# Sixteen copies of the experts' weights in DRAM, a new account of transfers in the build, and other constants of the order

## The chip, the core and the metric

The kernel runs on one core of one Trainium2 chip. The core has five engines, each with its own stream of instructions, which it works off in order: TensorE (matrix products; PE in the profile, PEld its weight loads), VectorE (DVE), ScalarE (ACT), GpSimd (POOL) and SyncE (SP), which here does nothing but issue transfers. Semaphores order the engines among each other. All transfers go out on SyncE's one queue and are carried by 16 DMA engines. The metric is the device time of one execution in microseconds (us); three executions of the kernel before took 1351.25 to 1354.19 us, median 1353.21.

## What is computed

The input is x, 8 sequences of 512 tokens with 128 channels, in fp32. Four blocks follow each other, each added to its input:

```python
x = x + mamba(layernorm(x))      # in-projection, short convolution, Silu, state scan, out-projection
x = x + ffn(layernorm(x))        # mixture of 8 experts
x = x + attention(layernorm(x))  # 16 heads of 8, chunks of 10 with 25 to the left
x = x + ffn(layernorm(x))        # the same mixture, with the same weights
```

The experts take most of the work. All eight compute every token, and their outputs are summed with a weight per token and expert:

```python
router_probs = softmax(x @ w_router);  gate_weights = softmax(x @ w_gating / 0.1)
h = silu(x @ w_gate[e]) * (x @ w_up[e]);  expert_out[e] = h @ w_down[e]      # 128 -> 512 -> 128
cw = router_probs * gate_weights;  cw = cw / (sum(cw) + 1e-9)
out = sum over e of expert_out[e] * cw[..., e]
```

## The kernel before

**The experts' stream.** `ffn_stream` runs over the pass k (0, 1), the sequence b (0 to 7), the expert e (0 to 7) and four chunks f of 128 of the 512 hidden channels. Tokens lie along the free dimension, 512 columns. For each chunk TensorE makes g and u, then, some chunks later, adds to y. Each of the three is made of three products (`matmul3`), since every operand is split into a high and a low part of type fp32r: high times high, low times high, high times low. `hidden` turns g and u into the operand of y: ScalarE takes Silu of g (h<-g), VectorE multiplies by u (h<-u,h), ScalarE or VectorE rounds to the high part (a cast, h<-h), and GpSimd or VectorE subtracts to get the low part (h<-h,h). g, u and y live in accumulator banks, of which the experts may hold six (MOST) and one more. While the function tables on ScalarE are those of the exponential, some of the first Silus are computed through tanh.

**The weights of the experts** in fp32 come in as "stage" tiles; ScalarE casts the high half and GpSimd (VectorE at times) subtracts for the low half, 24 tiles in all, during the first sequence.

**The first sequence** starts in two halves of 256 tokens (`passes`, `first_halves`): experts 0 to SPLIT-1 run first on the first half of the tokens, then on the second half, and the others on all 512. Before the first product TensorE makes "warm" products, which compute nothing; while it waits early in the stream it makes "idle" ones (`keep_warm`).

**The weights per token.** `ffn_prep` normalises the tokens, computes the logits (lps), turns them (rps), takes the exponential (pr), and has cw, 128 tokens by NT blocks by NE experts. It transposes cw on TensorE (cps), VectorE copies it out (cwt), SyncE stores it in DRAM (cwd), and `spreads` loads the row of one expert into all 128 partitions (cwb), two tiles in turn, one expert ahead. `weighted` then has VectorE multiply y by cwb, and GpSimd add that to acc. In the profile the names of such tiles have the letter f after the first part (cwd_f, pr_f).

**Other work beside the stream.** Mamba (tiles with an m), preparation of the experts, and attention (tiles with an a) are generators, called lanes. Each yields the engine that it needs next, and when it may go on.

**What sets the order.** The order of instructions is fixed while the kernel is built. `Clock` keeps an account of when each engine will be free: `cost` gives a duration for each operation and `run` adds it up; for a transfer `run` works out when the data will have landed. `Lanes.tick` takes, among all lanes that could go on by the account, the one with the earliest start, less an allowance. The constants steer this choice: SIDE and JOIN say how long a result must have been ready before work beside the stream takes TensorE; PRESS, HELD and SECOND are allowances; MAMBA_DUE and PREP_DUE say how early a lane counts as due; LATE bounds how long an exponential waits for a table that is already loaded; WARM_GAP is the gap by the account from which an idle product is put in, and WARM_TO how far into the stream (in sequences) this is done; SPLIT is told above. So any change of the account or of a constant can move instructions anywhere in the program, on all engines.

ScalarE's function tables hold sets of functions; a change between Silu, exponential and logarithm takes a table load (ACT_TABLE_LOAD). One part of the Mamba work loads the set with the exponential and the logarithm (mdelta, mdec).

Nearly all instructions are recorded by one helper, so that they share one line in the profile (269); they are told apart by the names of their tiles.

Of the kernel before, what the change touches and what calls it, by code (L numbers as in the profile page):

```python
# [8 lines left out]
F32 = mybir.dt.float32  # L9
# [9 lines left out]
P = 128  # L19
B, L, DIM = 8, 512, 128  # L20
NT = L // P
# [3 lines left out]
NE, FF = 8, 512  # L25
# [62 lines left out]

TABLES = {AF.Silu: (18,), AF.Exp: (0, 6), AF.Ln: (6,), AF.Tanh: (0, 18)}
INF = float("inf")  # L90
LAGS = {"T": 0.2, "A": 0.15, "V": 0.15, "P": 0.08}
TO_PE = 0.11
SAME = 0.125
AHEAD = 0.2
EDGE = 0.1
FIRST = 0.6
LATE = 0.3
SIDE = 0.5
JOIN = 2.0
JOIN_DUE = 0.0  # L100
JOIN_MAX = 6.0
JOIN_ATT = 3.0
# [2 lines left out]
OTHERS = 4  # L105
AT_FIRST = 7
WARM = 3.5
WARM_GAP = 0.25
WARM_TO = 1.5
SECOND = 0.2  # L110
PRESS = 0.4
HELD = 0.18
MAMBA_DUE = 0.9
PREP_DUE = 0.9
ATT_LEAD = 2.5
EARLY = 5
SPLIT = 4
EARLIEST = 2 * (DEPTH + 1)


# [8 lines left out]
class Clock:  # L129
# [105 lines left out]
    def run(self, key, name, out, args, kw, after, wait):  # L235
        c = self.cost(key, name, out, args, kw)
        start = max(self.end[key] + wait, after, self.now if key == "T" else self.based(key))
        if key == "T":
            if start > self.end["T"] + 2.4:
                self.cold = start  # L240
            if start < self.cold + 3.4:
                c *= 2
        if key in "VP" and self.shares(key, name, out, args):
            start = self.with_port(start, c)
        self.end[key] = start + c
        if key == "S":
            start = max(start, self.now)
            row = out.shape[-1]
            rows = out.shape[0] * size(out) // row
            each = max(row * (2 if out.dtype == BF16 else 4), 512)  # L250
            move = rows * each / 200e3
            self.moved = max(self.moved, start + c + 0.8) + move
            return self.moved + 0.6 + move
        self.hop[key] = start + c
        return start + c + LAGS[key]

# [121 lines left out]
def block_kernel(ctx: ExitStack, tc: tile.TileContext, x, pack_a, pack_b, pack_c, w_qkv, mask, mask_t, w_o,  # L378
# [4 lines left out]
    pe = Engine(nc.tensor, "T", clock)  # L383
# [3 lines left out]
    sp = Engine(nc.sync, "S", clock)  # L387

    const = ctx.enter_context(tc.tile_pool(name="const", bufs=1))
    dram = ctx.enter_context(tc.tile_pool(name="dram", bufs=1, space=DRAM))  # L390
    lnp = ctx.enter_context(tc.tile_pool(name="lnp", bufs=LNB))
    fp = ctx.enter_context(tc.tile_pool(name="fp", bufs=2))
# [10 lines left out]
    done = {}  # L403
# [73 lines left out]
    ident = const.tile([P, P], F32, name="ident")  # L477
# [545 lines left out]
    def ffn_prep(k, b, xc, t0=0, nt=NT):  # L1023

        nm = f"f{k}_{b}_{t0}"
        cols = slice(t0 * P, (t0 + nt) * P)

        def halves():
            if t0 == 0:
                ready[k, b] = [fp.tile([P, L], F32R, tag=f"xt{i}", name=f"xt{i}_{nm}") for i in range(2)], 0  # L1030
            return [t[:, cols] for t in ready[k, b][0]]

        if (k, b, t0) == (0, 0, 0):
            done["quiet"] = 0.0
        *_, xf = yield from normalised(xc, nm, halves, nt, t0 + nt == NT, quick=nt < NT, plain=True)
        if (k, b, t0) == (0, 0, 0):
            done.pop("quiet", None)
            done["calm"] = 0.0
        if t0 == 0:
            done["cw", k, b] = dram.tile([NT, NE, P], F32, tag="cwd", name=f"cwd_{nm}", bufs=3), 0.0, 0  # L1040
        cwd = done["cw", k, b][0]
        ready[k, b] = ready[k, b][0], cols.stop
        wr, = routes

        lps = yield from side([P, P], f"lps_{nm}")
        for t in range(nt):
            e = pe.matmul(lps[32 * t : 32 * t + 32], wr, xf[:, t * P : (t + 1) * P], start=True, stop=True)
        lanes.give("ln", e)
        yield "V"
        n = 32 * nt  # L1050
        lt = fp.tile([P, P], F32, tag="lt", name=f"lt_{nm}", bufs=1)
        freed(dve.tensor_copy(lt[:n], lps[:n]))
        yield "T"
        rps = yield from side([P, NT, 32], f"rps_{nm}")
        pe.transpose(rps.rearrange("p t c -> p (t c)")[:, :n], lt[:n], ident[:n, :n])
        yield "V"
        pr = fp.tile([P, 2 * NT, NE], F32, tag="pr", name=f"pr_{nm}")
        s8 = fp.tile([P, 2 * NT], F32, tag="s8", name=f"s8_{nm}")
        pr, s8 = pr[:, : 2 * nt], s8[:, : 2 * nt]
        prv = pr.rearrange("p (t s) e -> p t s e", s=2)  # L1060
        s8v = s8.rearrange("p (t s) -> p t s", s=2)
        logits = rps[:, :nt, : 2 * NE].rearrange("p t (s e) -> p t s e", s=2)
        dve.tensor_reduce(s8v, logits, AX.X, ALU.max)
        yield "V"
        freed(dve.tensor_tensor(prv, logits, s8v[:, :, :, None].to_broadcast([P, nt, 2, NE]), ALU.subtract))

        yield lambda: clock.table in TABLES[AF.Exp] or pos[0] >= k * B + b - LATE
        yield "A"
        act.activation(pr, pr, AF.Exp)
        if (k, b) == (0, 0) and t0:  # L1070
            clock.hold = clock.now


        yield "V"
        cw = fp.tile([P, NT, NE], F32, tag="cw", name=f"cw_{nm}")[:, :nt]
        s4 = fp.tile([P, NT], F32, tag="s4", name=f"s4_{nm}")[:, :nt]
        z = fp.tile([P, NT], F32, tag="z", name=f"z_{nm}")[:, :nt]
        dve.tensor_reduce(s8, pr, AX.X, ALU.add)
        pool.tensor_tensor(cw, prv[:, :, 0], prv[:, :, 1], ALU.mult)
        yield "V"  # L1080
        dve.tensor_reduce(s4, cw, AX.X, ALU.add)
        pool.tensor_tensor(z, s8v[:, :, 0], s8v[:, :, 1], ALU.mult)
        pool.tensor_scalar(z, z, 1e-9, 1.0, ALU.mult, ALU.mult)
        yield "P"
        pool.tensor_tensor(s4, z, s4, ALU.add)
        yield "V"
        dve.reciprocal(s4, s4)
        yield "P"
        pool.tensor_tensor(cw, cw, s4[:, :, None].to_broadcast([P, nt, NE]), ALU.mult)
        yield "T"  # L1090
        cps = yield from side([NT * NE, P], f"cps_{nm}")
        n = nt * NE
        pe.transpose(cps[:n], cw.rearrange("p t e -> p (t e)"), ident)
        yield "V"
        cwt = fp.tile([NT * NE, P], F32, tag="cwt", name=f"cwt_{nm}")
        freed(dve.tensor_copy(cwt[:n], cps[:n]))
        yield "S"
        e = sp.dma_start(out=cwd[t0 : t0 + nt].rearrange("t e p -> (t e) p"), in_=cwt[:n])
        done["cw", k, b] = cwd, e, cols.stop

    pos = [0.0]
# [21 lines left out]
    def ffn_stream():  # L1123
# [73 lines left out]
        def spreads():  # L1197

            for k in range(2):
                for b in range(B):  # L1200
                    todo = passes(k, b)
                    for i, (e, cs) in enumerate(todo):
# [3 lines left out]
                        cwd, there, _ = done["cw", k, b]  # L1206
                        yield "S", there
                        spread.append(e)
                        n = cs.stop - cs.start
                        cwb = fp.tile([P, L], F32, tag="cwb", name=f"cwb{k}_{b}_{e}_{cs.start}", bufs=2)[:, :n]  # L1210
                        state["cwb", (k, b, e, cs.start)] = cwb, sp.dma_start(
                            out=cwb.rearrange("p (t q) -> p t q", q=P),
                            in_=cwd[None, cs.start // P : cs.stop // P, e, :].to_broadcast([P, n // P, P]),
                        )

        def chunks(cs):
# [63 lines left out]
        for k in range(2):  # L1280
            for b in range(B):
                todo = passes(k, b)
                for n, (e, cs) in enumerate(todo):
# [8 lines left out]
                    for f in range(0, NFC, n_chunks):  # L1292
                        nm = f"{k}_{b}_{e}_{cs.start}_{f}"
# [567 lines left out]
```

## Time and profile before

| | before |
|---|---|
| median of three executions | 1353.21 us |
| the profiled execution, its own time | 1351.62 us |
| its span, first to last instruction | 1349.8 us |
| mean granted clock of TensorE | 0.996 |
| busy share PE / DVE / ACT / POOL | 98 / 77 / 71 / 70% |
| share of the 16 DMA engines' time | 33.9% |
| table loads on ScalarE | 125 (109 and 16 by line), 1.28 us each |
| broadcasts of the weights per token (cwb<-cwd_f) | 132: 124 of 256 KB, 8 of 128 KB |

A row of the profile names line, engine, operation, what it writes and reads with the shape, the count, then busy time and the mean length of one, then the idle time of the engine before it and what ended that. Products on TensorE overlap, so a row's length is not its cost; the cost of one is the distance to the start of the next. Idle products count as busy time. The chain of waits follows the work that ended last back to its beginning.

### The profile page before, as it was taken

How to read it: one execution, taken by the hardware profiler on the slowest of the kernel's cores; microseconds unless marked ns; L12 is line 12 of the kernel's file. 1: busy time of each engine (PE TensorE's matmuls, PEld its weight loads, DVE VectorE, ACT ScalarE, POOL GpSimd, SP SyncE). 2: the span in 40 equal slices, each digit the busy share in tenths (PEclk: the TensorE clock that was granted, in tenths of full speed). 3: DMA queues.
4: the chain of work that ended last, by engine and by line, in shares of the span. 5: the costliest groups of instructions: out<-in, count | busy, mean ns of one | idle time of the engine just before them, and what ended most of it. 6: DMA issues, size and time to landing. Idle time of an engine off the chain costs nothing.

```text
span 1349.8 us, 29533 instructions
## 1 busy us (share of the span) xinstructions
PE 1328.9 (98%) x10261; PEld 1053.3 (78%) x10261; DVE 1036.8 (77%) x3114; ACT 964.7 (71%) x1694; POOL 940.4 (70%) x1042
## 2 busy tenths in 40 slices
PE   7999999999999999999999999999999999999998
PEld 7877778788788877777777777777777777778887
DVE  6887888688888867898788887888888787855443
ACT  7768576867787556777777777777877767765654
POOL 5877576776767757666766767767677676777776
PEclk9999999999999999999999999999999999999999
DMA  3321304232112242344345444454544434222111
GB/s 126 95 72 38 87 24 101 62 81 73 45 48 56 63 85 54 73 97 118 79 103 111 99 106 100 104 109 89 118 91 104 119 71 88 61 69 55 40 40 40
DMA packets 230861, 107.75 MB, mean 80 GB/s; under 512 B 86417, under 2 KB 226616, under 8 KB 230712
## 3 DMA queue, kind: packets, MB, share of 16 engines
q1 hardware_dynamic: 230712, 105.87, 33.9%
q8 instruction: 81, 1.33, 0.4%
q14 instruction: 68, 0.56, 0.1%
HBM read 77.64 MB, written 27.79 MB: 78 GB/s over the span
## 4 chain that ended last, share of the span: by engine, by line
PE 89%; POOL 3%; ACT 3%; issue 3%; DVE 2%; DMA 0%; POOLq 0%; DVEq 0%
PE u L269 25%; PE y L269 25%; PE g L269 25%; PE ao L269 2%; PE aw L269 2%; PE as L269 2%; POOL h L269 1%; PE mo L269 1%; PE aqk L269 1%; ACT h L269 1%; DVE h L269 1%; PE mde L269 1%; PE aout L269 1%; PE yp L269 1%; ACT L269 1%
## 5 line engine op out<-in xcount | busy, mean ns | idle before, releaser
L269 POOL TENSOR_TENSOR h<-h,h 128x512 fp32r<-128x512 f32 x492 | 640.0, 1310 | 279.0 <-ACT h L269 219.4
L269 PE MATMUL u<-xt_f,wu 128*128 128x512 f32 (+1 forms) x1584 | 451.5, 395 | 3.5 <-ACT h L269 2.7
L269 PE MATMUL g<-xt_f,wg 128*128 128x512 f32 (+1 forms) x1584 | 448.3, 393 | 2.1 <-ACT h L269 1.9
L269 PE MATMUL y<-h,wd 128*128 128x512 f32 (+1 forms) x1584 | 445.5, 392 | 1.4 <-POOL h L269 0.8
L269 DVE TENSOR_TENSOR h<-u,h 128x512 f32<-128x512 f32 x420 | 285.9, 686 | 157.5 <-PE u L269 109.3
L269 ACT ACTIVATE h<-g 128x512 f32<-128x512 f32 x512 | 303.4, 597 | 123.2 <-PE g L269 100.1
L269 ACT CAST h<-h 128x512 fp32r<-128x512 f32 x437 | 268.4, 619 | 171.2 <-DVE h L269 169.6
L269 PEld LDWEIGHTS g<-xt_f,wg 128*128 128x128 f32 x1584 | 288.5, 189 | 70.3 <-ACT h L269 3.0
L269 PEld LDWEIGHTS y<-h,wd 128*128 128x128 f32 x1584 | 288.3, 188 | 70.2 <-POOL h L269 1.4
L269 PEld LDWEIGHTS u<-xt_f,wu 128*128 128x128 f32 x1584 | 286.6, 189 | 71.7 <-ACT h L269 4.1
L269 POOL TENSOR_TENSOR acc<-acc,cwb 128x512 f32<-128x512 f32 (+1 forms) x114 | 148.0, 1298 | 52.5 <-DVE cwb L269 33.8
L269 ACT ACT_TABLE_LOAD x109 | 139.8, 1283 | 24.7 <-PE g L269 23.2
L269 DVE CUSTOM_DVE_ANT_0 amasked<-as,maskq 128x60 f32<-128x60 f32 x640 | 95.4, 213 | 5.0 <-PE as L269 4.8
L269 DVE TENSOR_TENSOR cwb<-y,cwb 128x512 f32<-128x512 f32 (+1 forms) x116 | 77.5, 668 | 16.0 <-PE y L269 14.4
L269 DVE TENSOR_TENSOR apt<-aw,maskk 125x400 f32<-125x400 f32 (+2 forms) x160 | 88.1, 570 | 0.0
L269 DVE SCALAR_TENSOR_TENSOR h<-h,g 128x512 f32<-128x512 f32 x92 | 62.3, 681 | 27.0 <-ACT h L269 26.6
L269 ACT ACTIVATE apt<-apt 125x400 f32<-125x400 f32 (+2 forms) x160 | 81.5, 540 | 0.4
L269 DVE SCALAR_TENSOR_TENSOR h<-u,h 128x512 f32<-128x512 f32 x92 | 62.6, 683 | 3.3 <-PE g L269 0.5
L269 DVE DVE_READ_ACCUMULATOR2_ANT amx<- 128x1 f32 x640 | 52.1, 81 | 0.0
L269 DVE CAST h<-h 128x512 fp32r<-128x512 f32 x75 | 48.8, 651 | 1.2
L269 DVE COPY v<-avr 125x128 f32<-125x128 f32 (+2 forms) x40 | 25.7, 644 | 26.4 <-PE ao L269 26.4
L269 PEld LDWEIGHTS ao<-apt,v 125*32 125x32 f32 (+2 forms) x1280 | 27.4, 109 | 14.6 <-DVE h L269 4.4
(205 smaller groups left out, 1239.5 us busy)
## 6 DMA issues: line engine op xcount, KB each, us to landing
cwb<-cwd_f SPq DMA_DIRECT2D x124, 256.0 KB
aqd<-apc SPq DMA_DIRECT2D x32, 192.0 KB
ks<-aqd SPq DMA_DIRECT2D x48, 93.8 KB
x_fo<-x SPq DMA_DIRECT2D x16, 256.0 KB
aqd<-apc SPq DMA_DIRECT2D x32, 128.0 KB
x_f<-x SPq DMA_DIRECT2D x15, 256.0 KB
qs<-aqd SPq DMA_DIRECT2D x48, 75.0 KB
aod<-aos SPq DMA_DIRECT2D x24, 100.0 KB
```

The lines of the kernel that those rows point to most:

```text
L269: f(*args, **kw)
```

## The change

The weights of the tokens are stored in DRAM expert by expert, not block by block, so that the 512 weights of one expert are one piece of 2 KB. The store writes them sixteen times, and partitions 8r to 8r+7 of cwb read copy r. In the first sequence, which is prepared in two halves, there is one copy. To this end cw is laid out with the experts outside on chip as well, and the transpose follows that order.

In the build's account a transfer used to begin 0.8 us after its issue and to land 0.6 us and once more its moving time after its move; now it begins after 0.6 us and lands 0.8 us after its move. Eleven constants have other values.

```diff
+COPIES = 16
-LATE = 0.3
-SIDE = 0.5
-JOIN = 2.0
+LATE = 0.4
+SIDE = 0.7
+JOIN = 3.0
...
-WARM_GAP = 0.25
-WARM_TO = 1.5
-SECOND = 0.2
-PRESS = 0.4
-HELD = 0.18
-MAMBA_DUE = 0.9
-PREP_DUE = 0.9
+WARM_GAP = 0.5
+WARM_TO = 2.5
+SECOND = 0.1
+PRESS = 0.2
+HELD = 0.05
+MAMBA_DUE = 1.0
+PREP_DUE = 0.8
...
-SPLIT = 4
+SPLIT = 5
...
-            self.moved = max(self.moved, start + c + 0.8) + move
-            return self.moved + 0.6 + move
+            self.moved = max(self.moved, start + c + 0.6) + move
+            return self.moved + 0.8
...
-            done["cw", k, b] = dram.tile([NT, NE, P], F32, tag="cwd", name=f"cwd_{nm}", bufs=3), 0.0, 0
+            copies = COPIES if nt == NT else 1
+            done["cw", k, b] = dram.tile([copies, NE, NT, P], F32, tag=f"cwd{copies}", name=f"cwd_{nm}", bufs=3), 0.0, 0
...
-        cw = fp.tile([P, NT, NE], F32, tag="cw", name=f"cw_{nm}")[:, :nt]
+        cw_rows = fp.tile([P, NE * NT], F32, tag="cw", name=f"cw_{nm}")[:, : NE * nt]
+        cw = cw_rows.rearrange("p (e t) -> p t e", e=NE)
...
-        pe.transpose(cps[:n], cw.rearrange("p t e -> p (t e)"), ident)
+        pe.transpose(cps[:n], cw_rows, ident)
...
-        e = sp.dma_start(out=cwd[t0 : t0 + nt].rearrange("t e p -> (t e) p"), in_=cwt[:n])
+        if nt == NT:
+            e = sp.dma_start(
+                out=cwd.rearrange("r e t p -> (e t) r p"), in_=cwt[:, None, :].to_broadcast([n, COPIES, P])
+            )
+        else:
+            e = sp.dma_start(out=cwd[0, :, t0 : t0 + nt, :], in_=cwt[:n])
...
-                            out=cwb.rearrange("p (t q) -> p t q", q=P),
-                            in_=cwd[None, cs.start // P : cs.stop // P, e, :].to_broadcast([P, n // P, P]),
+                            out=cwb,
+                            in_=cwd[:, None, e, cs.start // P : cs.stop // P, :]
+                            .rearrange("r o t q -> r o (t q)")
+                            .to_broadcast([cwd.shape[0], P // cwd.shape[0], n]),
```

## The prediction

> **What bounds the kernel now.** I read the page's busy times first, then busy time by stage, then TensorE and ScalarE in order of time where a stage falls short.
>
> ```profile
> PE 1328.9 (98%) x10261; PEld 1053.3 (78%) x10261; DVE 1036.8 (77%) x3114; ACT 964.7 (71%) x1694; POOL 940.4 (70%) x1042
> L269 ACT ACT_TABLE_LOAD x109 | 139.8, 1283 | 24.7 <-PE g L269 23.2
> ```
>
> TensorE sets the time; the others have a quarter of the span free. So a transfer or an operation elsewhere counts only where TensorE stands. The stages, first whole, then the opening in detail (columns: stretch, its length, then PE, PEld, DVE, ACT, POOL busy, granted clock, DMA share, GB/s):
>
> ```profile
> 0.00:40.00 40.00, 32.34 (x212) 28.64 (x213) 27.31 (x71) 26.53 (x57) 22.12 (x33) 0.96 0.41 126
> 300.00:500.00 200.00, 200.00 (x999) 160.18 (x998) 163.36 (x324) 140.31 (x241) 132.15 (x134) 1.00 0.26 62
> 900.00:1100.00 200.00, 199.62 (x2108) 155.88 (x2099) 166.62 (x619) 152.40 (x275) 140.18 (x165) 1.00 0.47 102
> ...
> 51.60:59.10 7.50, 7.44 (x50) 5.66 (x48) 5.04 (x11) 6.69 (x12) 5.71 (x6) 1.00 0.34 90
> 67.00:71.00 4.00, 2.85 (x12) 1.47 (x11) 3.55 (x13) 3.92 (x6) 1.37 (x2) 0.98 0.02 7
> 71.00:76.00 5.00, 4.88 (x22) 4.00 (x21) 3.91 (x9) 4.99 (x12) 4.27 (x6) 0.68 0.25 63
> ```
>
> From 300 us on TensorE is full and nothing is to be had but cheaper products. The slack lies in the opening, and busy time hides it, because "idle" products (fillers that compute nothing) count as busy. In order of time (start, length, engine, what):
>
> ```profile
> 51.63 1.17 PE L269 MATMUL idle<-sel 128*128 128x256 f32 x4
> 55.94 1.17 PE L269 MATMUL idle<-sel 128*128 128x256 f32 x6
> 68.38 2.14 PE L269 MATMUL idle<-sel 128*128 128x256 f32 x5 [0.86 <-DVE cwt_f L269]
> 70.58 1.46 PE L269 MATMUL u<-xt_f,wu 128*128 128x256 f32 x6
> ```
>
> To size it I count useful work. In the chain three 512-column products take 0.70 us (0.233 each), six 256-column ones 0.72 (0.12 each); the others go by the median from start to start. The first gate product starts at 34.31 us, the first of the second half of the tokens at 59.10: 24.8 us for 20.7 of work, 4.1 lost. From there to expert 5 at 99.59: 40.5 us for 31.8 of work, 8.7 lost. What holds TensorE at 67 to 71 is ScalarE:
>
> ```profile
> 61.09 1.28 ACT L269 ACT_TABLE_LOAD   x1
> 62.39 0.23 ACT L269 ACTIVATE pr_f<-pr_f 128x32 f32<-128x32 f32 x1
> 62.64 1.28 ACT L269 ACT_TABLE_LOAD   x1
> 63.93 0.60 ACT L269 ACTIVATE h<-g 128x512 f32<-128x512 f32 x1
> 64.55 1.28 ACT L569 ACT_TABLE_LOAD   x1
> 65.84 1.30 ACT L269 ACTIVATE mdelta<-mdelta 128x512 f32<-128x512 f32 x2
> 67.17 1.95 ACT L269 ACTIVATE mdec<-mdelta,nega 128x512 f32<-128x512 f32 x3
> 69.15 0.72 ACT L269 ACTIVATE mdelta<-mdelta,nega 128x512 f32<-128x512 f32 x1
> 69.89 1.28 ACT L269 ACT_TABLE_LOAD   x1
> 71.19 1.57 ACT L269 ACTIVATE h<-g 128x512 f32<-128x512 f32 x3
> ```
>
> Four table loads in ten microseconds: only one Silu of the experts runs between 60 and 71 us, the accumulator banks stay full, TensorE starves, and its clock falls to 0.68 for the next 5 us.
>
> **The change, part by part.** The programs of both versions, engine by engine, give the counts.
>
> *Transfers of the weights.* 132 broadcasts of 256 KB become 133 whose pieces are 2 KB (1 KB for half rows), not 512 B. In the landing events of the trace the 512-byte form takes 4.86 us (median) after its issue, a broadcast of the same size in 2 KB pieces (aall_over) 2.93; I expect about 3. In 15 of the 16 preparations the store grows from 16 to 256 KB: from 1.7 us towards the 2.5 of the 256 KB store avd. SP issues these in order, so cwb of expert 0 and whatever is queued behind it come about 1 us later, once per sequence. Who waits? VectorE waits for cwb 0.5 us in the whole span, and TensorE's waits for transfers are three rows of 0.7. So the gain is 0 to 2.1 us, the loss at most 1 us of SP per sequence, hidden by the next cwb being loaded one expert ahead. I take 0. If that cover were gone, each of the 15 could lose 1 us; the 0.5 us row says it is not.
>
> The Trainium skill, "DMA: Bandwidth & Descriptors" (the rule on using all 16 engines), says that an outermost dimension under 16, such as a leading broadcast, confines a transfer to that many engines. It would speak against fewer copies; sixteen just meets it, and no run here shows the other case.
>
> *First product (A).* GpSimd forms the low half of a weight from 28.93 for 1.30 us and only at 30.31 starts the norm that VectorE had ready at 29.57. In the new program ScalarE casts the first weight of that group ahead of four exponentials and a table load, not behind them (GpSimd had idled 8.62 us for this cast, up to 26.36), and the last cast of the group comes 0.8 us sooner for GpSimd: 0.7 gained, all that VectorE allows. The filler ahead of the first gate product (33.89 to 34.31) goes: 0.4. A = -1.1; bounds 0 and -1.7.
>
> *Filling the wait for the second half (B).* SPLIT 5 runs expert 4 on the first half too: 36 products at 0.12, 4.3 us of work before the second half is needed, in the place of 14 fillers, of which 4 are left. The price: 36 products of 0.233 become 72 of 0.12, +0.3. Expert 4's weights are needed some 35 us earlier (its first product started at 86.7); their casts move ahead, and one low half goes from GpSimd (1.29) to VectorE (0.69 for an operation of this form). Of 4.1 us lost I take half: B = -2.1 + 0.3 = -1.8; bounds -3.8 and +0.3.
>
> *Behind it (C).* The exponential of the second half's router moves into the stretch whose table already holds it: two of the four loads go, 2.57 us of ScalarE. Against that, two weight casts and one h cast (3 x 0.52) and this exponential (0.23) now stand in the Silu-free stretch, which grows from 6.64 us (64.55 to 71.19) to 6.64 + 1.8 = 8.4. But ScalarE enters it less late: the two Silus ahead of it were 5.7 us apart (58.21 and 63.93), and now nothing stands between them. GpSimd does the two h's ahead of three weights (3.8 us) instead of behind two. Of 8.7 us I take 3.0; bounds -8 and +1.8.
>
> *Clock.* The gap before a filler is put in doubles, to 0.5. At 68.38 to 70.58 five fillers ran, and the clock fell to 0.68 all the same, so these fillers bought nothing: 0. The Trainium skill, "TensorE: Matmul & The Clock Gate" (Part 1), has a window of about 3.4 us of low activity before half rate; by it single gaps of 0.5 are harmless too, and the sum would be the same.
>
> *Order of the rest (D, E).* Table loads go from 125 to 131, but 19 to 15 in the first two sequences and 106 to 116 after them. Ten at 1.28 us are 12.8 us of ScalarE, where it is busy 70 to 76% and TensorE is full: taken at 0. "ScalarE: Activation LUTs" of the skill (What ACT_TABLE_LOAD costs) adds a drain, 2.66 us in all; the rows show 1.30 from the load's start to the next operation (61.09 to 62.39), so the row holds. The stalls at 174 and 263 us (1.9 and 1.6) stand at Silu-free stretches of ScalarE; by the rows' lengths the old program has eight of over 4 us from expert 6 of the first sequence on, the new one ten. D = +1.0, half a stall for each of the two; bounds -4 and +5. Changes between 512-column products and small ones fall from 104 to 99 and, with the row-tiled ones, from 79 to 76, at 0.1 to 0.15 us: E = -1.0 with the cheaper neighbours, bounds 0 and -2. The end of the program is the same on all engines.
>
> **Sum.** -1.1 - 1.8 - 3.0 + 1.0 - 1.0 = -5.9 us on the profiled execution's 1351.62 (span 1349.8): 1345.7. That execution is 1.6 below the median of the three runs, 1353.21, so 1347.3.
>
> **Rivals.**
> 1. *ScalarE's Silu-free stretches decide (slower).* Stock for TensorE lasts some 4 us: the stretch of 6.3 us at 169.68 to 175.95 cost 1.9 us and then a slow clock. If the 8.4 us stretch keeps B and C from coming, and half of the ten later loads come through (6.4 us), the sum is -1.1 + 0.3 - 1.0 + 6.4 = +4.6: 1357.8. For it: six loads more, one stretch longer. Against: no stall at any of the 106 later loads but 0.85 us at 521. It decides from the fourth later load on that comes through whole (-1.8 + 4 x 1.28 = +3.3).
> 2. *GpSimd sets the pace of the opening (no change).* Between 71 and 90 us the chain of waits runs through GpSimd, which has 24 weight halves of 1.29 us to make. Then B and C only move the wait: -1.1 + 0.3 - 1.0, 1351.4.
> 3. *All of the slack comes (much faster):* -1.7 - 3.8 - 8 - 2 = -15.5: 1337.7.
> 4. *The copies don't speed the transfers up.* Same account, since they count at 0.
>
> **How the numbers follow.** My sum 0.50, rival 1 0.20, rival 2 0.19, rival 3 0.11; rival 4 lies inside all. 0.2% is 2.7 us, about what a measurement of this kernel can tell. Faster 0.61 (my sum, rival 3), same 0.19, slower 0.20. The range, 1340.5 to 1356.5, cuts off half of rival 3 and the upper half of rival 1; for my sum alone it would be 1342 to 1351.
>
> **What would show it.** After: the first gate product near 33 us; one or two fillers before the second half; two table loads, not four, around the second Mamba sequence and no 3 us hole there; expert 5 of the first sequence some 6 us earlier; from 300 us on a full TensorE. Wrong: a hole of over 3 us at the first router weights of the second half, new waits of TensorE for ScalarE's h after 100 us, or waits for cwb on VectorE.

## The result, and the profile after

The changed kernel takes 1356.34 us (median of ten executions, 1354.43 to 1357.14), the kernel before 1352.84 on the same chip (ten executions, 1350.55 to 1354.84). The ratio is 1.0024, with a 95% interval of 1.0016 to 1.0033: some 3.3 us slower, where I had forecast 6 us faster. The profiled execution of the changed kernel took 1357.14 us (span 1355.4), that of before 1351.62, so the two traces lie 5.5 us apart, 2 us more than the medians.

From the page of the changed kernel, the busy times and the group of table loads:

```profile
PE 1329.7 (98%) x10267; PEld 1055.1 (78%) x10267; DVE 1042.7 (77%) x3125; ACT 966.0 (71%) x1684; POOL 942.8 (70%) x1047
L270 ACT ACT_TABLE_LOAD x114 | 146.3, 1283 | 29.2 <-PE g L270 26.0
```

The shares are the same as before. What differs shows only by stage (stretch, its length, then PE, PEld, DVE, ACT, POOL busy, granted clock, DMA share, GB/s; changed kernel):

```profile
36.00:40.00 4.00, 2.36 (x13) 1.76 (x12) 3.96 (x9) 0.60 (x1) 2.58 (x3) 0.90 0.48 138
40.00:44.00 4.00, 3.94 (x21) 3.45 (x21) 2.82 (x10) 1.32 (x3) 0.41 (x2) 0.67 0.23 59
72.00:78.00 6.00, 2.30 (x19) 2.09 (x18) 4.84 (x18) 5.78 (x10) 4.97 (x9) 0.90 0.36 110
78.00:84.00 6.00, 6.00 (x26) 5.45 (x27) 4.44 (x8) 4.51 (x10) 5.25 (x8) 0.54 0.01 3
900.00:1100.00 200.00, 198.07 (x2042) 153.36 (x2041) 162.06 (x633) 148.87 (x258) 139.33 (x171) 1.00 0.45 103
```

Two holes in the opening, each with a slow clock behind it, and TensorE no longer full between 900 and 1100 us: 198.07 of 200, against 199.62 before. In order of time (start, length, engine, what), the two holes:

```profile
35.90 0.87 PE L270 MATMUL u<-xt_f,wu 128*128 128x256 f32 x6
38.30 0.83 PE L270 MATMUL idle<-sel 128*128 128x256 f32 x2 [1.52 <-DVE mst L270]
39.18 1.65 PE L270 MATMUL g<-xt_f,wg 128*128 128x256 f32 x6
...
73.26 0.88 PE L270 MATMUL g<-xt_f,wg 128*128 128x256 f32 x6
77.84 0.80 PE L270 MATMUL idle<-sel 128*128 128x256 f32 x2 [3.70 <-DVE s_f L270]
78.48 1.65 PE L270 MATMUL u<-xt_f,wu 128*128 128x256 f32 x6
```

Six 256-column products that take 0.72 us at full clock take some 1.45 behind each hole. I now count useful work in both traces alike: each product at the median distance to the next one of its kind over both traces, warm and idle products at nothing; what is left of a stage is lost.

| stage | us before | us after | work before | work after | lost before | lost after |
|---|---|---|---|---|---|---|
| to the first gate product | 34.31 | 35.09 | 8.2 | 8.2 | 26.1 | 26.9 |
| to the first of the second half of tokens | 24.79 | 30.77 | 19.5 | 23.2 | 5.3 | 7.6 |
| to expert 5 of the first sequence | 40.49 | 37.06 | 31.0 | 27.5 | 9.5 | 9.6 |
| to expert 4 of sequence 3, second pass | 894.30 | 893.42 | 843.8 | 842.9 | 50.5 | 50.5 |
| to sequence 5, second pass (996 to 1130 us after) | 128.74 | 133.33 | 119.5 | 119.7 | 9.2 | 13.7 |
| to the last product | 223.94 | 222.52 | 214.0 | 213.6 | 9.9 | 8.9 |

So the traces lose 2.3 us more in the first half of the tokens and 4.4 us more in sequences 3 and 4 of the second pass. How a stage divides into work and loss depends on how the kinds of products are told apart: other ways give 1.4 to 2.8 us and 3.7 to 4.4 us for these two, and a change of the work behind expert 5 of either sign. The starts of the products don't depend on it: expert 5 of the first sequence starts at 102.92 us, not at 99.59, so 3.3 us later, where A, B and C together had it 5.9 earlier; from there to the end it takes 2.3 us more, where D and E together had 0.

### The profile page after: what moved, and what is told of

Its sections match the earlier page's. It is cut to its first block, busy times and chain, and to the rows that moved or that the text cites. A ratio compares the mean times of both kernels' runs of the same rounds, so it can differ in the third digit from the quotient of the medians.

```text
span 1355.4 us, 29498 instructions
## 1 busy us (share of the span) xinstructions
PE 1329.7 (98%) x10267; PEld 1055.1 (78%) x10267; DVE 1042.7 (77%) x3125; ACT 966.0 (71%) x1684; POOL 942.8 (70%) x1047
## 4 chain that ended last, share of the span: by engine, by line
PE 86%; DVE 4%; ACT 3%; DMA 3%; POOL 2%; issue 2%; SPq 0%; POOLq 0%; ACTq 0%; DVEq 0%
PE g L270 24%; PE u L270 24%; PE y L270 24%; PE ao L270 2%; PE aw L270 2%; PE as L270 1%; PE mo L270 1%; DVE h L270 1%; POOL h L270 1%; ACT h L270 1%; PE aqk L270 1%; DMA x_a<-x 1%; PE mde L270 1%; PE yp L270 1%; DMA aall_over<-aoverd 1%
## 5 line engine op out<-in xcount | busy, mean ns | idle before, releaser
L270 ACT CAST h<-h 128x512 fp32r<-128x512 f32 x432 | 265.6, 618 | 194.3 <-DVE h L270 192.6
L270 ACT ACT_TABLE_LOAD x114 | 146.3, 1283 | 29.2 <-PE g L270 26.0
L270 DVE TENSOR_TENSOR cwb<-y,cwb 128x512 f32<-128x512 f32 (+1 forms) x117 | 77.5, 663 | 12.1 <-PE y L270 11.7
L270 PEld LDWEIGHTS ao<-apt,v 125*32 125x32 f32 (+2 forms) x1280 | 27.5, 109 | 14.2 <-issue 5.1
```

What stands on the lines that cost most here:

```text
L270: f(*args, **kw)
```

## The experiments

Theory 1: the new order of instructions makes the loss, not the transfers. Within it, theory 2 put the loss in the opening, its rival in the later table loads.

### The copies alone, and the order alone

`order_only` is the counterpart of `copies_only`: old store and loads, with the account told the new shapes. Every engine's order is that of before, or that of the changed kernel.

```diff
 # kernel before, with the new layout of cwd and cw, and for the account:
+                plan=Shape(n, P),          # store: the old shape
+                            plan=Shape(P, n // P, P),   # load: the old shape
-            return self.clock.run(self.key, name, out, args, kw, after, wait)
+            return self.clock.run(self.key, name, plan or out, args, kw, after, wait)
```

> The kernel before with the sixteen copies and the one-piece loads of the weights, while the account of the build is given the old shapes, so that every instruction stands where it stood before. Theory 1 (the order alone makes the loss): the same time as before, within 1.5 us, though cwb lands in about 3.4 us, not 4.9. Rival (the copies make it: the 256 KB store holds up SyncE's queue and other transfers): 2 to 4 us slower than before. A gain of up to 2 us would say that VectorE's and TensorE's waits for transfers in the profile of before were real.

Measured: 1352.62 us, ratio to before 0.9992 (0.9983 to 1.0001). By the landing events cwb lands 3.43 us after its issue (median; 4.86 before), the store of cwd in 2.53 (1.72 before). Of TensorE's stalls, those behind the first gate product are before's, shifted by some 2.2 us; the largest is still there with the same releaser (start, length, what; kernel with the copies alone):

```profile
70.61 2.14 PE L276 MATMUL idle<-sel 128*128 128x256 f32 x5 [0.86 <-DVE cwt_f L276]
```

The transfers became faster as said, and TensorE gained nothing by it that can be measured.

> The changed kernel's order of instructions, kept exactly, with the old store and the old loads of 512-byte pieces. Theory 1 (the order alone makes the loss): 3 to 4 us slower than before, as the changed kernel is. Rival (the copies make it): the time of before within 1 us. If the new order depends on the faster loads, it is slower still than the changed kernel, by over 1.5 us.

Measured: 1359.79 us, 1.0051 (1.0039 to 1.0063). The order alone is slower, more so than with the copies (1.0024). So in the new order, which was laid out by an account of quicker loads, the copies do bring some 3.5 us; in the old one nothing that can be measured. This is the third possibility of the expectation.

### Account and constants

```diff
 # opening_back: changed kernel with      # steady_back: changed kernel with
+WARM_GAP, WARM_TO = 0.25, 1.5            +LATE, SIDE, JOIN = 0.3, 0.5, 2.0
+SECOND, SPLIT = 0.2, 4                   +PRESS, HELD = 0.4, 0.18
                                          +MAMBA_DUE, PREP_DUE = 0.9, 0.9
 # consts_back: changed kernel with all eleven of them old
 # account_back: changed kernel with
+            self.moved = max(self.moved, start + c + 0.8) + move
+            return self.moved + 0.6 + move
```

> The changed kernel with SPLIT, WARM_GAP, WARM_TO and SECOND at their old values; all else is as changed. Theory 2 (the opening makes the loss, through the idle of TensorE at 36.5 us and the hole of 3.9 us at 73.9 us with the slow clock behind it): the time of before or up to 3 us faster, first gate product of expert 5 of the first sequence near 99.6 us. Rival (the later order makes it: ten table loads more after the first two sequences, small stalls from 1000 us on): still 2 to 4 us slower than before, with the loss behind 200 us.

> The changed kernel with LATE, SIDE, JOIN, PRESS, HELD, MAMBA_DUE and PREP_DUE at their old values; the new SPLIT, fillers and SECOND stay. Theory 2 (the opening makes the loss): still 3 us or more slower than before, expert 5 of the first sequence near 103 us. Rival (the later order makes it): within 1.5 us of before, with expert 5 still near 103 us and the rest some 3 us quicker than in the changed kernel.

> The changed kernel (copies and new account of transfers) with all eleven constants at their old values: 131 table loads, 31 idle products. If the account alone makes the worse order: 3 us or more slower than before. If the constants do: within 2 us of before. If every new order is a draw, and the old constants were chosen for the old account: 5 to 30 us slower, as the two kernels with half of the constants were.

> The changed kernel with the old account of transfers, and with the copies and the eleven new constants: 124 table loads, 17 idle products. If the account alone makes the worse order: within 2 us of before. If the constants do: 3 us or more slower. If every new order is a draw: 5 to 30 us slower.

| account | opening constants | other constants | us | ratio to before (95%) |
|---|---|---|---|---|
| old | old | old | 1352.84 | 1 |
| new | old | old | 1367.86 | 1.0112 (1.0099 to 1.0125) |
| new | new | old | 1368.21 | 1.0110 (1.0097 to 1.0123) |
| new | old | new | 1382.93 | 1.0220 (1.0207 to 1.0233) |
| old | new | new | 1360.27 | 1.0051 (1.0036 to 1.0066) |
| new | new | new | 1356.34 | 1.0024 (1.0016 to 1.0033) |

(All but the first row with the copies.) Every mixture is slower than both whole sets, by 4 to 30 us. Of theory 2 and its rival only "3 us or more slower" for `steady_back` came, by far more than was meant; `consts_back` (15 us slower) and `account_back` (7 us) fit the third possibility of their expectations, that every new order is a draw. With the opening's constants put back, the trace is 32.1 us longer than before's, and 28.1 of that lie behind the start of sequence 2 (217.1 us, before 213.1), when its last idle product (160.8 us) and the split sequence are past: a small change early gives another order everywhere. The parts of this change can't be priced by putting single ones back. What follows therefore keeps an order and changes one thing in it.

### The stretch without Silu, in the order of before

```diff
 # in the call of an engine's operation (ScalarE)
+            if name == "activation" and args[0].name.startswith("pr_f0_0_2"):
+                self.later = args
+            else:
+                f(*args, **kw)
+                if name == "activation" and self.later:
+                    self.real.preload_act_table_set("natural_log_exp_and_others")
+                    self.real.activation(*self.later)
```

> The kernel before with one move on ScalarE: the exponential of the router's second half in the first sequence (pr_f) goes behind the Silu that follows it, into the table that Mamba's stretch loads anyway, so that two of the four table loads between 61 and 70 us go; VectorE, TensorE and GpSimd keep their order, and pr_f comes some 0.6 us later. It is the part of step C that saves loads, alone. Theory C (ScalarE's stretch without Silu holds TensorE's banks there): the stretch begins 2.6 us sooner, the idle at 67 to 71 us shrinks to under 1.5 us, the slow clock behind it goes, and the kernel is 2 to 5 us faster than before. Rival (something else holds TensorE there, VectorE's or GpSimd's queue): under 1 us gained.

Measured: 1352.52 us, 1.0008 (0.9998 to 1.0017): nothing gained, and theory C's 2 to 5 us don't come. TensorE in order of time, kernel with the move:

```profile
68.44 1.61 PE L273 MATMUL idle<-sel 128*128 128x256 f32 x5 [0.86 <-DVE cwt_f L273]
...
78.06 0.38 PE L273 MATMUL idle<-sel 128*128 128x256 f32 x1 [1.72 <-ACT h L273]
```

GpSimd of the same kernel (start, length, what, idle before and releaser):

```profile
71.32 0.20 POOL L273 TENSOR_SCALAR va_m<-mv_m 128x4 f32<-128x4 f32 x1 [2.98 <-DVE mv_m L273]
...
73.28 1.28 POOL L273 TENSOR_TENSOR wg<-stageg,wg 128x512 fp32r<-128x512 f32 x1
74.51 1.29 POOL L273 TENSOR_TENSOR wu<-stageu,wu 128x512 fp32r<-128x512 f32 x1
76.11 2.49 POOL L273 TENSOR_TENSOR h<-h,h 128x512 fp32r<-128x512 f32 x2 [0.32 <-ACT h L273]
```

Up to there the mechanism is right in part: ScalarE's stretch ends 2.6 us sooner, the first hole is 0.7 us shorter, and the clock between 72 and 78 us is 1.00, not 0.81. The wait of 0.86 us for cwt_f is the same, though, and the five idle products behind it have their fixed place in the order, so in this run most of that hole stays whatever ScalarE does. But at 76 us TensorE now waits 1.72 us, where it waited 0.41, and the gain is gone by 81 us. GpSimd stands idle for Mamba's statistics until 71.32, then makes the next norm and two low halves of weights, and comes to h only at 76.11. What the stretch gave, GpSimd's queue took, as these rows read: the mechanism of my rival 2. The same move without the idle products was not run.

### The stretch without Silu, in the new order

ScalarE of the changed kernel, in order of time:

```profile
68.98 1.28 ACT L570 ACT_TABLE_LOAD   x1
...
75.29 0.21 ACT L270 ACTIVATE pr_f<-pr_f 128x32 f32<-128x32 f32 x1
75.52 1.28 ACT L270 ACT_TABLE_LOAD   x1
76.82 1.58 ACT L270 ACTIVATE h<-g 128x512 f32<-128x512 f32 x3
```

VectorE of the changed kernel over the same microseconds:

```profile
75.54 0.19 DVE L270 TENSOR_REDUCE s_f<-pr_f 128x4 f32<-128x32 f32 x1 [0.64 <-ACT pr_f L270]
75.64 0.69 DVE L270 SCALAR_TENSOR_TENSOR mbx<-mdec,mbx 128x512 f32<-128x512 f32 x1
76.60 1.19 DVE L270 TENSOR_TENSOR_SCAN mst<-mdec,mbx 128x512 f32<-128x512 f32 x1
```

From the last Silu (ends 67.94) to the next, 8.9 us pass. TensorE goes on at 77.84, as the scan ends at 77.79: by the order of the banks the idle product takes the one that Mamba's mbx held until the scan had read it. The profile's releaser, s_f, is only the last small operation that ended on VectorE before that. In `order_only`, `after_noload` and `after_pr` too that product starts 0.05 to 0.06 us after this scan ends.

```diff
+                if name == "activation" and self.ahead is not None and args[0].name.startswith("mdelta"):
+                    self.real.activation(self.ahead, self.ahead, AF.Exp)     # pr_f first (after_pr)
+    act.moved = {"wd5_0_": nc.gpsimd.tensor_copy, "wg6_0_": nc.gpsimd.tensor_copy,
+                 "h00_0_0_256_0_": nc.vector.tensor_copy}                    # and these (after_stretch)
```

> The changed kernel with one exponential moved on ScalarE: pr_f of the second half runs first in Mamba's stretch, right behind its table load, not last. VectorE's row that waits for it (s_f) stands ahead of the row that feeds Mamba's scan, and the scan releases the bank that TensorE waits for at 73.9 us. Theory (VectorE in order behind a late pr_f lengthens the hole): the hole of 3.9 us shrinks by 0.5 to 1.2 us. Rival (ScalarE's stretch alone sets it): the hole is the same or 0.2 us longer. The time as a whole: 0 to 1.5 us less than the changed kernel.

> The changed kernel with pr_f moved first as in the run above, two weight casts that stand ahead of Mamba's table load given to GpSimd, and the h cast inside the stretch given to VectorE; everything else in its order. ScalarE's stretch without Silu, 67.9 to 76.8 us, becomes some 1.6 us shorter (three casts of 0.52). Theory (the stretch makes the hole at 73.9 us): the hole shrinks from 3.9 us to 1 to 2.5 us, and the time is 1.5 to 4 us less than the changed kernel, at or under that of before. Rival (VectorE or GpSimd sets the pace there): the hole stays over 3 us, or the same time is lost a few us later.

Measured: `after_pr` 1355.19 us, 1.0030 (1.0019 to 1.0040); `after_stretch` 1354.69, 1.0019 (1.0009 to 1.0029). By distance over the median the hole at 73.8 us shrank from 3.86 to 3.11 with pr_f first, and to 1.39 with the three casts moved as well: the theory holds for the hole. But with the short stretch 1.9 us of it come back at once as a wait of cps_f for GpSimd's cw_f, since GpSimd now has two casts more ahead of it. The time of the whole moved by less than can be told from the changed kernel's.

### The idle products

```diff
-                t, = take("experts", [[P, L]], ["idle"])
-                freed(pe.matmul(t[:, :HALF], sel[:, 0], sel[:, : HALF // P], start=True, stop=True), "experts")
+                del lanes.free["bank"][0]
+                lanes.give("bank", clock.run("T", "matmul", warm[:, :HALF], ..., 0.0, 0.0) + TO_PE)
```

> The changed kernel without its ten idle products; the order of all else is kept (the idle products are counted in the account but not issued). Theory (they only wait for the same bank as the product behind them and cost their own length): holes at 36.5 and 73.9 us begin and end as before, 0 to 1 us gained. Rival 1 (taking a bank in turn, they make the holes themselves): 2 us or more gained. Rival 2 (they hold up the granted clock): 1 us or more lost behind the holes.

> The kernel before without its thirty idle products, order of all else kept. Theory (idle products cost a little of their own length and a bank's turn, and hold up no clock): 0.5 to 2.5 us less than before. Rival (they keep the granted clock up in the opening): 1 us or more slower, with lower granted clock between 60 and 90 us.

Measured: `after_nofill` 1353.84 us, 1.0010 (1.0000 to 1.0019); `before_nofill` 1354.08, 1.0003 (0.9994 to 1.0012). The holes keep their lengths (1.67 and 1.69; 3.86 and 3.87), so the fillers don't make them. Without them the changed kernel is some 1.9 us better, with intervals that just overlap (1.0000 to 1.0019, 1.0016 to 1.0033). In the profiles the clock from 40 to 44 us is 1.00, not 0.67, and from 78 to 84 us 0.72, not 0.54; but the execution of `order_only`, which has the same idle products and the same two holes, shows 1.00 and 0.72 as well, so these clocks don't show that the idle products cost them. In the order of before, thirty of them cost or bring nothing that can be measured.

> The changed kernel with the shorter stretch without Silu (pr_f first, two casts to GpSimd, one to VectorE) and without the idle products, both as in the runs above. If the two gains add, it is some 2.5 us less than the changed kernel and within 0.1% of before on either side; if both come from the same clock drops in the opening, it is no better than the kernel without idle products alone.

Measured: 1353.25 us, 1.0006 (0.9997 to 1.0014); expert 5 starts 65.3 us after the first gate product, as before (65.3; 67.8 in the changed kernel). With these two the time is some 2.4 us under the changed kernel's, near the sum of the two gains. What is left in the profile lies between 990 and 1130 us (13.3 us lost there; 9.2 before).

### The table loads of the second pass

The programs show which of the router's exponentials (pr_f) stand alone between two loads, and which ride in attention's stretch of exponentials. In the second pass three of eight stand alone in the order of before (sequences 0, 3, 7), seven in the new one (all but 6).

```diff
 # after_noload
+            if name == "activation" and args[0].name[:7] in ("pr_f1_1", ..., "pr_f1_5"):
+                f(args[0], args[1], AF.Silu)
 # before_loads, ahead of the Silu of experts 0, 3, 6 of sequences 1 to 5
+                    self.real.preload_act_table_set("natural_log_exp_and_others")
```

> The changed kernel, in its own order, but in the second pass the router's exponentials (pr_f) of sequences 1 to 5 are computed with the Silu function instead: they stood alone, each between a pair of table loads, and with Silu those ten loads go and nothing else moves. (The weights per token, and so the output, are wrong for these sequences; the amount of work is the same.) In the order of before four of these five stand inside attention's stretch of exponentials and cost no load. Theory L (these lone pairs hold ScalarE and with it TensorE's banks, which is the loss of some 4 us between 995 and 1130 us): 2.5 to 5 us less than the changed kernel, the loss between 995 and 1130 us mostly gone. Rival (table loads under a full TensorE are covered, as my step D had it; the waits there come from attention's masks on VectorE): within 1 us of the changed kernel.

> The kernel before, in its own order, with fifteen pairs of table loads more (a load of the exponential's set ahead of a Silu, and the load back) in the second pass, sequences 1 to 5, ahead of experts 0, 3 and 6. It prices a lone pair where TensorE is full. Theory L: 0.3 to 0.8 us for a pair on average, 5 to 12 us in all. Rival (covered): under 0.15 us for a pair, under 2 us in all. If every load came through whole it would be 38 us.

Measured: `before_loads` 1364.46 us, 1.0085 (1.0071 to 1.0099): 11.5 us for fifteen pairs, 0.77 (0.64 to 0.89) for a pair. Table loads under a full TensorE are not covered here. `after_noload` 1355.24 us, 1.0015 (1.0003 to 1.0027): about 1 us better than the changed kernel, not 2.5 to 5. One stall, 0.71 us at 1112, went with its lone pair; the loss from sequence 3 to 5 fell from 13.7 to 12.7 us only.

### Loads that begin late

In the group of loads shown above ScalarE stood idle 29.2 us ahead of loads, 26.0 of it waiting for g. The load needs no g; but the build puts it in front of Silu without a place of its own, and in the program it carries Silu's wait. ScalarE of the changed kernel:

```profile
1040.02 1.28 ACT L270 ACT_TABLE_LOAD   x1 [1.12 <-PE g L270]
1041.31 0.60 ACT L270 ACTIVATE h<-g 128x512 f32<-128x512 f32 x1
```

```diff
+SETS = {0: "exp_and_others", 6: "natural_log_exp_and_others", 18: "silu_and_others"}
+        if func in TABLES and self.clock.table not in TABLES[func]:
+            self.real.preload_act_table_set(SETS[TABLES[func][0]])
             f(*args, **kw)
```

> The kernel before in its own order and with the same 125 table loads, but each load is an instruction of its own that waits for nothing, put in front of the operation that needs it; so it runs while ScalarE waits for TensorE's g, not after it. In the profile of before ScalarE stands idle 24.7 us ahead of loads, 23.2 of it waiting for g. Theory E (a load costs TensorE time because it begins only when g is there): the time falls by 3 to 12 us. Rival (TensorE has other work for that time): within 1.5 us of before.

> The changed kernel in its own order with the same 131 table loads, each waiting for nothing, as in the run above. Theory E: it gains at least as much as the kernel before does, since its idle time ahead of loads is 29.2 us against 24.7, and the waits for g and u between 995 and 1130 us (3 us more than before) shrink by 1 us or more. Rival: within 1.5 us of the changed kernel, and those waits stay.

> The kernel before, with all its table loads waiting for nothing and with the same fifteen pairs of loads more as in the run with pairs, these too waiting for nothing. Theory E (the price of a pair is the load back that begins only when g is there): under 0.35 us for a pair, under 5 us in all. Rival (ScalarE's 2.57 us themselves are the price): 0.6 to 0.9 us for a pair, 9 to 13 us in all, as without it.

> The changed kernel with all three: the shorter stretch without Silu, no idle products, and table loads that wait for nothing; the order is otherwise its own. If the gains add (1.0024, less 0.0018 for the first two together, less 0.0016 for the third) it ends at 0.999 of before, some 1 to 2 us faster than it. If they overlap, it stays between 1.000 and 1.001.

The same place in the changed kernel with loads that wait for nothing, ScalarE in order of time:

```profile
1034.40 0.97 ACT L277 ACTIVATE apt<-apt 127x408 f32<-127x408 f32 x2
1035.39 1.28 ACT L270 ACT_TABLE_LOAD   x1
1036.68 0.60 ACT L277 ACTIVATE h<-g 128x512 f32<-128x512 f32 x1
```

The group of loads on that kernel's page:

```profile
L270 ACT ACT_TABLE_LOAD x114 | 146.3, 1283 | 2.0
```

The load now stands behind attention's last exponential, and TensorE's wait for the next g (0.5 us at 1041.96 in the changed kernel) is gone.

| kernel | us | ratio to before (95%) |
|---|---|---|
| before, loads early | 1352.36 | 0.9999 (0.9990 to 1.0007) |
| changed, loads early | 1353.48 | 1.0008 (0.9998 to 1.0019) |
| before, loads early, fifteen pairs more | 1360.95 | 1.0057 (1.0037 to 1.0076) |
| changed, short stretch, no idle products | 1353.25 | 1.0006 (0.9997 to 1.0014) |
| the same and loads early | 1351.54 | 0.9989 (0.9976 to 1.0002) |

In the order of before the 23 us of waiting ahead of loads cost TensorE nothing (theory E falls there). In the new order early loads bring some 2 us, twice (1.0024 to 1.0008, and 1.0006 to 0.9989; each time the intervals overlap), and the three remedies add up, to the time of before or a little under it; that it beats before is not shown, since the interval reaches 1.0002. The price of an extra pair falls from 0.77 (0.64 to 0.89) to about 0.5 us (7.8 us between 0.9999 and 1.0057, over fifteen; some 0.3 to 0.7 by the intervals). It lies between what theory E and its rival said: perhaps a third was the late start, which these intervals hardly tell, and the larger part is ScalarE's time.

Where early loads help is less clear. With them alone the loss from sequence 3 to 5 falls from 13.7 to 11.7 us, and the second hole of the opening from 3.86 to 3.02; with all three remedies the stage loses 13.9, and the gain lies before it. Other executions of the new order lose 12.7 to 14.2 there.

Over the nine profiled executions in the new order (the changed kernel and eight with something changed in it), from the first gate product to expert 5 takes 64.6 to 67.8 us, against 64.7 to 65.3 in five of the order of before: in the opening the loss comes and goes, with the clock among other things (65.8 in `order_only`). Sequences 3 and 4 of the second pass take 131.3 to 133.9 us, against 128.6 to 128.8: this stage is longer every time.

What makes it longer is only partly settled. Attention's steps fall otherwise (256 value products, ao, in it, not 224), and TensorE waits there for banks that VectorE (amx, apt) or ScalarE (h) still reads, 2.1 us of idle time ahead of g and u products against 0.1, and no single one is over 0.6 us. One cause that I didn't test is the waiting for transfers. VectorE's waits for x_a, the kernel before and the changed kernel (us in total, times, longest):

```profile
DVE st_a L269 <- DMA x_a<-x: 0.6, 1, 0.6
DVE st_a L270 <- DMA x_a<-x: 9.6, 6, 1.8
```

In the changed kernel one of these waits stands 2.7 us ahead of TensorE's longest in this stage:

```profile
1000.41 0.49 DVE L270 BATCH_NORM_STATS2 st_a<-x_a 128x6 f32<-128x128 f32 x2 [1.72 <-DMA x_a<-x]
1003.14 0.93 PE L270 MATMUL u<-xt_f,wu 128*128 128x512 f32 x3 [0.58 <-DVE amx L270]
```

In all VectorE waits 21 us for transfers in the changed kernel and 7 before. At 1092 us, where VectorE waits 1.46 us for x_f, TensorE waits 0.2 us in the changed kernel; in `order_only` these are 2.54 and 1.3 us. No run takes these waits away, and most of them stand in the stretch before this stage, which takes no longer than in the kernel before; so what they cost is not shown.

## Why the prediction was wrong

*Transfers: 0, measured 0* in the order of before (0.9992). That nobody waits for cwb was read rightly. I hadn't asked what the new order would need: there the copies bring some 3.5 us. Nor did the sum have a term for the other transfers, which the new account lets land one moving time sooner, 1.3 us for 256 KB by its formula: the order then puts VectorE's operations ahead of their data, and it waits 21 us for transfers, not 7.

*A, first product earlier: -1.1, measured +0.8, and no gain within its scatter.* With one and the same order the first gate product started at 34.2 to 37.3 us in the profiled executions, by when the first loads came. From the first of Mamba's broadcast products (mbx, 15.2 and 15.9 us) to it, 19.2 us pass before and 19.1 after. The step said what GpSimd and ScalarE gain; but VectorE's chain (clip, x_m, statistics) came later.

*B, SPLIT 5 fills the wait: -1.8, measured +2.3* in this trace. The fillers went, as said (30 to 10 in all), and 72 half products for 36 whole ones cost what was said. The step failed in what is late next: the new order has Mamba's first scans on VectorE end 3.1 us behind the first gate product, not 2.0, and 1.7 us of hole at 36.5, two fillers and a slow clock came into the stage whose wait was to be filled.

*C, two loads less at the second half: -3.0, measured +0.1.* The two loads went, and the stretch without Silu is 8.9 us (I had 8.4). Counted from the first gate product of the second half, ScalarE ends the last Silu ahead of it after 2.1 us, not 5.4, and comes back to Silu after 11.0, not 12.1: it was less late, as I had said. But TensorE's next u comes after 12.6 us, not 11.5. The step failed in the wait: I took TensorE to wait for ScalarE's Silu, and it waits for a bank that Mamba's scan on VectorE reads last, behind mdec and pr_f from that same stretch. And the saving was worth nothing by itself: done alone in the old order it brought nothing, with GpSimd's queue next.

*D, the rest: +1.0, measured +3.4* (from expert 5 on, lost 69.6 before and 73.1 after; bounds -4 and +5; other ways of counting give D +0.8 to +2.7 and E -0.4 to +1.5; together they are +2.3 by the starts, forecast 0). The failed term is the ten later loads, "12.8 us of ScalarE, where it is busy 70 to 76% and TensorE is full: taken at 0". A pair costs 0.77 us where TensorE is full, in the order of before. By that price the five additional pairs would be 3.8 us, an estimate from another order; taking five lone pairs away brought about 1 us. So of the 4.4 us in the stage that is longer every time, loads explain about 1 by that one run, and the rest is open.

*E, fewer changes of product kinds: -1.0, measured -1.1* by the table (work from expert 5 on, 1177.3 and 1176.2), which other ways of counting don't bear out.

*Clock and fillers: 0.* Fillers buy no clock, as read; in the new order taking them out brought some 1.9 us, hardly clear of the scatter. But that the clock counts 0 in the sum didn't follow from it. Over its ten executions the changed kernel was granted 0.9937 of the clock on average, the kernel before 0.9966 (seventeen executions beside `copies_only`): by the spans, 8.5 and 4.6 us of lost clock, a difference about as large as the whole loss. Between the first gate product and 300 us the trace of before has two stretches of 3.4 us at half the clock (near 71 and 177 us), that of the changed kernel four (near 39, two near 77, near 251). How much of it reaches the time is not shown: `before_nofill` lost 7.1 us of clock, before beside it 4.9, and took no longer that can be measured.

Of the rivals, the first came nearest: slower, with a hole of over 3 us at the second half's router weights and loads that come through. Its "half of the ten" (6.4 us) was too much, and it set B at +0.3, so that 1357.8 was near 1356.3 partly by chance. That 1356.34 lies just inside my range (up to 1356.5) is owed to the half of this rival in it; by my sum alone it ended at 1351. The weight of 0.20 was too little: A, B and C, which I took as gains, each rested on one engine being ahead, and none on the engine that would then be last.

## What to carry to other kernels

Where an order comes out of a list scheduler, a change of its account or constants is a new draw everywhere, and parts of it can't be judged by putting them back one at a time: keep the order and change one operation in it. Before a saved load or operation on one engine is booked as a gain, follow the in-order queue of each other engine through the same microseconds, and look which bank the next product takes and who reads it last. Busy 70% beside a full TensorE does not make an engine's extra work free: price it by adding some. And where an account of transfers is shortened, look at the waits for all transfers, not only for the one that was made faster.

## What was not expected of the hardware

The same stall had different clocks. In the new order TensorE stands 1.74 us at 248 us in every profiled execution; the stretch from 252 to 260 us of the changed kernel (columns as in the first table by stage):

```profile
252.00:260.00 8.00, 8.00 (x38) 6.05 (x38) 7.87 (x21) 4.54 (x10) 6.50 (x8) 0.86 0.00 0
```

The same stretch of the kernel with the short stretch without Silu:

```profile
252.00:260.00 8.00, 8.00 (x37) 6.40 (x36) 8.00 (x20) 4.86 (x11) 6.70 (x8) 1.00 0.01 4
```

By the granted clock from 247 to 260 us (0.88 and 0.86 in the two parts up to and from 252; 1.00 and 1.00) the slow clock cost the first some 1.7 us, the other nothing. The Trainium skill, "TensorE: Matmul & The Clock Gate" (Part 1), says that the window in which activity is judged runs free and that the count of slow products changes from run to run; these rows agree. It gives about 3.4 us as the window; the stretches at half the clock in these traces last 3.4 us or a multiple of it, and a stall of half that was enough at times. So one trace of each kernel can't tell 2 us.

VectorE's clip of mdec (128x256, mdec<-mdec,cap) took 0.34 us at 31.92 and 34.58 in the changed kernel, but 1.05 at 28.96 and 1.18 at 35.04: these two ended 0.15 us after the weight's low half that GpSimd was making. Over all 29 clips the median rose from 480 ns before to 826 after. "SBUF — State Buffer" of the skill (Who interferes with whom) has VectorE's two-port operations and GpSimd share a port pair, whoever comes later being blocked for the whole instruction; these rows agree, though the clip at 31.92 was not held while GpSimd ran its small rs_f (31.79, 0.71 us); the new order met it more often. In both traces all 13 clips of 128x512 that began while GpSimd ran no operation of 512 columns took 0.46 to 0.49 us; of those that began during one (11 of 21 before, 18 of 21 after) 25 of 29 took 0.6 to 1.6 us.
